# A two-layer graph attention and expert kernel: second-layer score terms over DRAM instead of TensorE, dense expert weights kept in SBUF

## The chip, the cores and the metric

The kernel runs on one core of a Trainium2 chip. The metric is the device time of one execution in microseconds (us). An execution with the hardware profiler gives a trace; its span runs from the first to the last instruction, and the execution's own time is a little longer. Engines: PE is TensorE (PEld its weight loads), DVE is VectorE, ACT is ScalarE, POOL is GpSimd, SP is SyncE, which here only issues DMAs. L523 is line 523 of the kernel before.

## The reference, cut to what matters

The input x is 64 batches of 256 rows of 256 numbers (float32). Two layers follow one another, each a graph attention and a feed-forward part, both added to x behind a layer norm.

```
x = x + gat0(layernorm(x))            # 4 heads of 64, slope 0.2, elu
x = x + layernorm(x) @ Wf.T + bf
x = x + gat1(layernorm(x))            # 1 head of 256, slope 0.01, relu
x = x + moe(layernorm(x))             # 8 experts, the best 2 of each row
```

In a graph attention h = x @ W, each row i has two numbers s_i = h_i.a1 and d_i = h_i.a2, and

```
e_ij = leaky_relu(s_i + d_j), masked by adj;   out_i = softmax_j(e_ij) @ h
```

The expert part gives each row the sum of two experts' gelu(x @ w1[e] + b1[e]) @ w2[e] + b2[e], weighted by a softmax over the two, plus the row itself.

## The kernel before, in words

Because exp(leaky_relu(s + d)) is the larger of two products of exponentials, the scores need no exponential per pair (i, j): for each source row j (a partition) a multiplication by masked factors and a maximum with a term that belongs to i and lies along the free dimension. The terms of the 256 rows i must therefore stand as a row of 256 numbers on all 128 partitions, while they are computed as a column, one per partition. This turn and spread is what the change is about.

Batches. A batch goes through `batch_layers` (L594): transposition, projection (L469), first-layer scores (`scores`, L559), weighted sum (`attended`, L576, PE pv L584), first feed-forward (PE pf L660, then DVE L667), second-layer projection (`projected1`, L497), scores (`scores1`, L520), weighted sum, second residual (DVE L694), norm, base rows (the residual and norm that the experts add to), router logits (PE pl L748). The first 61 batches are routed: in chunks (11 of 4 batches, 7 of 2, 3 of 1) their normed rows are sent by GpSimd's indirect DMAs (L1066) into regions of DRAM, one per expert. Full pairs of 128 rows of one expert (129 in all) are then loaded by SyncE (xr L906, xt L917, the expert's weights we L935), turned by VectorE (sT L117), go through PE ph L968, ACT hT L974, PE py L983, DVE y L993 and ACT y L961, and GpSimd adds them to the output by two indirect DMAs (L1004). Each pair's two scatters wait for the landing of the two before (L1001). The last three batches are dense: all 8 experts are computed for them (`dense_expert`, L1022), first for batch 61, then for 62 and 63 together, and each of these 16 jobs loads its expert's weights (L1026) into the same 7 buffers "we" as the pairs.

Order. The order on every engine is written out by a small planner (L1241). A job is a generator; each of its pieces ends with `yield rank`. In one step of the planner all active jobs go on by one piece, smallest rank first; a negative rank means that the next piece still belongs to this step. A new batch begins every three steps, so several batches are in flight at different places, and a rank decides what stands ahead of what on each engine. Engines work strictly in this order, and so does each DMA queue: a DMA that waits holds up all that are behind it on its queue.

The turn before. In the first layer (from batch 1) VectorE turns blocks of 32x32 of the exponentials (ut, L537), a DMA writes them to DRAM as one row (L621), and another reads that row onto all partitions (L554), into a part of the buffer that the maxima are then written to; from batch 18 (`SETTLED`) both are on SyncE's queue. In the second layer TensorE does it: two transpositions (L523) of the column, spread to 128 columns, give the row in PSUM, and the two maxima L528 read it there. Both stand at rank 25 of the step behind the projection; the weighted sum follows at rank 40 of the next step.

The values' scaling is DVE L485 (first layer, rank 24). It needs ACT's exponentials q L477.

Of the kernel before, what the change touches and what calls it, by code (L numbers as in the profile page):

```python
# [9 lines left out]
F32 = mybir.dt.float32  # L10
I32 = mybir.dt.int32
AF = mybir.ActivationFunctionType
ALU = mybir.AluOpType
AX = mybir.AxisListType

P = 128
# [5 lines left out]
def rows_to_all(ap: bass.AP, n: int) -> bass.AP:  # L22

    return bass.AP(tensor=ap.tensor, offset=ap.offset, ap=[[0, P], [1, n]])
# [3 lines left out]
def kernel(  # L28
# [17 lines left out]
    nc = tc.nc  # L46
    B, N, D = x.shape
# [3 lines left out]
    KT = D // P  # L51
    NT = N // P
# [16 lines left out]
    ROW = D + 4  # L69
# [3 lines left out]
    io = ctx.enter_context(tc.tile_pool(name="io", bufs=2))  # L73
    work = ctx.enter_context(tc.tile_pool(name="work", bufs=2))
    small = ctx.enter_context(tc.tile_pool(name="small", bufs=4))
    keep = ctx.enter_context(tc.tile_pool(name="keep", bufs=1))
    psum = ctx.enter_context(tc.tile_pool(name="psum", bufs=2, space=bass.MemoryType.PSUM))

    def bank(name, shape):
        t = psum.tile([P, 2 * D], F32, tag="bank", name=name, bufs=8)  # L80
        n = 1
        for s in shape:
            n *= s
        t = t[:, :n]
        if len(shape) == 2:
            t = t.rearrange("p (a b) -> p a b", a=shape[0])
        elif len(shape) == 3:
            t = t.rearrange("p (a b c) -> p a b c", a=shape[0], b=shape[1])
        return t
# [22 lines left out]
    S = 32  # L112
    G = P // S
# [15 lines left out]
    SETTLED = CHUNKS[0] + CHUNKS[1] + CHUNKS[2] + CHUNKS[3] + 2  # L129


    ident = const.tile([P, P], F32, tag="ident", name="ident")
# [138 lines left out]

    C_B1, WROW = KT * D, KT * D + 64
    WBUFS, XBUFS, YBUFS = 7, 5, 9
    wpack = tc.dram_tile([E, P, WROW], F32, name="wpack")
    w2s = const.tile([P, E, KT * D], F32, tag="w2s", name="w2s")
# [41 lines left out]
    def once(work):  # L319
# [14 lines left out]
        out=tri, in_=tri, pattern=[[1, P]], base=0, channel_multiplier=-1,  # L334
# [157 lines left out]
    for i in range(2):  # L492
        t = keep.tile([P, NT, D + 1], F32, tag=f"q1_{i}", name=f"q1_{i}")
# [3 lines left out]
    def projected1(xT, rstd, b):  # L497

        q = q1s[b % 2]
        pqs = []  # L500
        for t in range(NT):
            pq = bank("pq", [D + 3])
            for k in range(KT):
                nc.tensor.matmul(  # L504
                    pq, xT[:, k, t * P : (t + 1) * P], wx1[:, k, :],
                    start=(k == 0), stop=(k == KT - 1),
                )
            pqs.append(pq)
        ex = small.tile([P, NT, 3], F32, tag="ex1", name="ex1")
        for t, pq in enumerate(pqs):  # L510
            nc.scalar.activation(ex[:, t, :], pq[:, D:], AF.Exp, scale=rstd[:, t : t + 1])  # L511
            nc.scalar.activation(
                q[:, t, :D], pq[:, :D], AF.Copy, scale=rstd[:, t : t + 1]
            )
        me = work.tile([P, NT, N], F32, tag="me", name="me", bufs=1)
        for j in range(NT):
            nc.scalar.activation(me[:, j, :], masks[1][:, j, :], AF.Copy, scale=ex[:, j, 0:1])
        return q, ex, me

    def scores1(ex, me):  # L520
        pd = bank("pd", [N])
        for t in range(NT):
            nc.tensor.transpose(  # L523
                pd[:, t * P : (t + 1) * P], ex[:, t, 1:2].to_broadcast([P, P]), ident
            )
        z = work.tile([P, NT, N], F32, tag="z1", name="z1", bufs=1)
        for j in range(NT):
            nc.vector.scalar_tensor_tensor(  # L528
                z[:, j, :], pd, ex[:, j, 2:3], me[:, j, :], op0=ALU.max, op1=ALU.mult
            )  # L530
        return [z[:, j, :] for j in range(NT)]

    def send_terms(q, b):


        ut = small.tile([P, S], F32, tag="ut", name="ut", bufs=1)
        nc.vector.transpose(  # L537
            ut.rearrange("p (t h w) -> p t h w", t=NT, h=H), q[:, :, :, HD - 1 : HD + 3]
        )
        ud = tc.dram_tile([S, S], F32, name=f"terms_{b}")  # L540
        ud = ud.rearrange("c r -> (c r)").rearrange("(c p) -> c p", p=P)
        return ut, ud
# [51 lines left out]
    def batch_layers(b, c0, xng, lg):  # L594
# [23 lines left out]
        if b:  # L618
            ut, ud = send_terms(q, b)
            yield -31  # L620
            terms_queue(b).dma_start(  # L621
                out=ud.rearrange("c (g r) -> g c r", g=G),
                in_=ut[2 : P : S // (NT * H), :],
            )
            yield -52
        z = work.tile([P, NT, NT, H, P], F32, tag="z4", name="z4", bufs=2)
# [17 lines left out]
        ex = work.tile([P, NT, D], F32, tag="e", name="e", bufs=1)  # L644
# [21 lines left out]
        for t in range(NT):  # L666
            nc.vector.scalar_tensor_tensor(  # L667
                x2[:, t, :], pf[:, t, :], rstd[:, t : t + 1], x1b[:, t, :],
                op0=ALU.mult, op1=ALU.add, accum_out=sums[:, t : t + 1],
# [6 lines left out]
        xT = transposed(x2)  # L676
        yield 20
        q, ex, me = projected1(xT, rstd, b)
        yield 25
        z = scores1(ex, me)  # L680
        yield 40
        pvs, rinv = attended(
            q[:, :, None, :], 1, lambda j, h, t: z[j][:, t * P : (t + 1) * P]
# [9 lines left out]
        for t in range(NT):  # L693
            nc.vector.scalar_tensor_tensor(  # L694
                x2[:, t, :], x2[:, t, :], 1.0, rel[:, t, :],
                op0=ALU.mult, op1=ALU.add, accum_out=sums[:, t : t + 1],
# [36 lines left out]
        if not dense:  # L733
            d = nc.sync.dma_start(
                out=out_rows[b * N : (b + 1) * N, :].rearrange("(t p) d -> p t d", p=P), in_=base
# [18 lines left out]
            dense_batch[b] = dict(base=base, xT=xT)  # L754

    XNG = 8
    dense_batch = {}

    def dense_home(b):

# [203 lines left out]
    def hidden(xT, we):  # L964
        ph = bank("ph", [KT, PAIR])
        for f in range(KT):
            for k in range(KT):
                nc.tensor.matmul(  # L968
                    ph[:, f, :], we[:, k * D + f * P : k * D + (f + 1) * P], xT[:, k, :],
                    start=(k == 0), stop=(k == KT - 1),  # L970
                )
        hT = work.tile([P, KT, PAIR], F32, tag="hT", name="hT", bufs=5)
        for f in range(KT):
            nc.scalar.activation(  # L974
                hT[:, f, :], ph[:, f, :], AF.Gelu, bias=we[:, C_B1 + f : C_B1 + f + 1]
            )
        return hT

    def product(hT, e):
        py = bank("py", [2, D])  # L980
        for t in range(2):
            for f in range(KT):
                nc.tensor.matmul(  # L983
                    py[:, t, :], hT[:, f, t * P : (t + 1) * P],
                    w2s[:, e, f * D : (f + 1) * D].rearrange("p e c -> p (e c)"),
                    start=(f == 0), stop=(f == KT - 1),
                )
        return py
# [33 lines left out]
    def dense_expert(e, group):  # L1022

        yield 90
        we = io.tile([P, WROW], F32, tag="we", name="we", bufs=WBUFS)
        nc.sync.dma_start(out=we, in_=wpack[e])  # L1026
        yield 40
        for b in group:
            own = dense_batch[b]
            yield 35  # L1030
            hT = hidden(own["xT"], we)
            yield -85
            py = product(hT, slice(e, e + 1))
            for t in range(NT):
                for add in (py[:, t, :], b2s[:, e, :]):
                    nc.vector.scalar_tensor_tensor(
                        own["base"][:, t, :], add, own["w"][:, t, e : e + 1],
                        own["base"][:, t, :], op0=ALU.mult, op1=ALU.add,
                    )
            if e == E - 1:  # L1040
                begin(store_dense(b), 99)

    def store_dense(b):

        own = dense_batch[b]
        yield 99
        d = nc.sync.dma_start(
            out=out_rows[b * N : (b + 1) * N, :].rearrange("(t p) d -> p t d", p=P),
            in_=own["base"],
        )  # L1050
        tc.declare_no_dep(d.ins, query=SYNC, group="out", reason="no row is added to here")
        tc.add_to_no_dep_group("out", d.ins)
        nc.sync.nop()
# [6 lines left out]
    def begin(job, rank):  # L1060
        active.append([rank, len(order), job])
        order.append(job)
# [126 lines left out]
    def route_dense(b, lg):  # L1189

        c = len(CHUNKS) + 1 + b - ROUTED
        ohs, ed = in_one(top_two(c, NT, lg, chunk_tile([NT], "first", c)))
        yield 75
        two = chunk_tile([2, NT], "two", c)
        nc.scalar.activation(two[:, 0], ed, AF.Tanh, scale=-0.5)
        second_weight(two[:, 1], two[:, 0])
        nc.vector.tensor_tensor(two[:, 0], two[:, 0], two[:, 1], ALU.add)
        w = chunk_tile([NT, E], "wd", c, DENSE)
        nc.vector.tensor_tensor(
            ohs, ohs, two[:, :, :, None].to_broadcast([P, 2, NT, E]), ALU.mult  # L1200
        )
        nc.vector.tensor_tensor(w, ohs[:, 0], ohs[:, 1], ALU.add)
        dense_batch[b]["w"] = w
        for group in GROUPS:
            if b == group[-1]:
                dense_jobs.extend(
                    (len(group), lambda e=e, g=group: dense_expert(e, g)) for e in range(E)
                )
# [109 lines left out]
```

## Time and profile before

| | |
|---|---|
| median of 3 runs | 1486.39 us (1485.4 to 1491.55) |
| profiled execution, its own time | 1489.83 us |
| its span | 1488.0 us, mean granted TensorE clock 0.985 |
| busy: PE / PEld / DVE / ACT / POOL | 1420.1 / 1264.0 / 1232.9 / 1006.5 / 864.6 us |
| DMA | 236.10 MB, mean 159 GB/s |
| SyncE's queue (q1 with ACT's share) | 157.90 MB, 42.1% of 16 engines |
| GpSimd's queue (q0) | 66.33 MB, 23.9% |
| we<-wpack | 145 loads of 288 KB |
| pd<-ident,ex (L523) | 128 transpositions, mean 278 ns, 26.2 us |
| z<-pd,ex,me (L528) | 128 maxima, mean 460 ns, 53.8 us |

How to read it: busy time is the sum of what an engine's instructions took. TensorE's matmuls are pipelined and the ends of the pieces are modelled, so that pieces overlap; the distance from one start to the next tells what a piece holds. In lines of the timeline the columns are the start in us from the span's start, the length in us, engine, line, operation, output<-inputs, shape, count, and in brackets the idle time of the engine ahead of it with what ended it. SPq is SyncE's DMA queue; the length of its lines is the time of issue, not of the transfer. In lines of waits the columns are who waited for whom, the us in total, how often, and the longest.

### The profile page before, as it was taken

The page shows a single profiled execution, that of the slowest core. Times are in us where ns is not written, and L with a number is a line of the kernel's source. Part 1 is how long each engine was busy: PE and PEld are TensorE (multiplying, and loading weights), DVE is VectorE, ACT ScalarE, POOL GpSimd, SP SyncE. Part 2 cuts the span into 40 slices and gives each one's busy share as a digit, 9 for nine tenths or more (in the row PEclk, how much of TensorE's full clock was granted, in tenths as well). Part 3 has the DMA queues.
Part 4 walks back from the last instruction along what each step waited for, and adds up shares of the span by engine and source line. Part 5 has one row for each costly group of instructions (what it writes and reads, how often), then busy time and mean ns, then how long its engine had stood idle before and what let it go on. Part 6 is the DMA issues. An engine that isn't in the chain of part 4 may idle for free. (4 is left out here: it accounts for less than half of the span.)

```text
span 1488.0 us, 29865 instructions
## 1 busy us (share of the span) xinstructions
PE 1420.1 (95%) x8138; PEld 1264.0 (85%) x8138; DVE 1232.9 (83%) x4320; ACT 1006.5 (68%) x2389; POOL 864.6 (58%) x851
## 2 busy tenths in 40 slices
PE   6899999999999999999999999999999999899994
PEld 5688888898999999899999989888888888778883
DVE  7689999988898889899888989998888888765442
ACT  1377667577777777777777787777777878643330
POOL 2122446455857676666758585776666668544444
PEclk9899999999999999999999999999999999999998
DMA  4832243567878777787877687768877786988743
GB/s 128 227 98 86 89 130 117 146 172 153 199 171 193 161 177 170 171 185 180 190 156 190 147 193 168 190 164 186 193 158 172 153 173 128 213 201 150 152 66 49
DMA packets 354081, 236.10 MB, mean 159 GB/s; under 512 B 246260, under 2 KB 316156, under 8 KB 353916
## 3 DMA queue, kind: packets, MB, share of 16 engines
q1 hardware_dynamic: 301000, 157.90, 42.1%
q0 software_dynamic: 48864, 66.33, 23.9%
q10 hardware_dynamic: 4052, 9.98, 2.3%
q8 instruction: 67, 1.10, 0.3%
q14 instruction: 98, 0.80, 0.2%
HBM read 146.00 MB, written 88.09 MB: 157 GB/s over the span
## 5 line engine op out<-in xcount | busy, mean ns | idle before, releaser
L1004 POOL DMA_INDIRECT out_dram<-y,xt x258 | 415.6, 1611 | 214.6 <-issue 54.6
L584 PE MATMUL pv<-q,z 128*128 128x65 f32 (+1 forms) x2560 | 363.7, 297 | 0.7 <-DVE z L570 0.3
L584 PEld LDWEIGHTS pv<-q,z 128*128 128x128 f32 x2560 | 331.2, 193 | 13.3 <-DVE z L570 1.3
L1066 POOL DMA_INDIRECT xs<-xng,pos x244 | 256.3, 1050 | 65.2 <-issue 57.7
L983 PE MATMUL py<-w2s,hT 128*128 (+1 forms) x1224 | 282.9, 382 | 4.7 <-ACT hT L974 4.5
L983 PEld LDWEIGHTS py<-w2s,hT 128*128 128x128 f32 x1224 | 229.7, 191 | 37.2 <-ACT hT L974 7.4
L570 DVE SCALAR_TENSOR_TENSOR z<-z,q,mask 128x256 f32<-128x256 f32 x504 | 231.5, 482 | 15.5 <-DMA z<-terms 6.5
L968 PE MATMUL ph<-sT,we 128*128 128x256 f32 x1032 | 241.4, 383 | 1.6 <-DVE sT L117 0.9
L968 PEld LDWEIGHTS ph<-sT,we 128*128 128x128 f32 x1032 | 195.6, 192 | 28.7 <-DVE sT L117 1.4
L961 ACT ACTIVATE y<-y,w 128x256 f32<-128x256 f32 x258 | 113.4, 499 | 119.4 <-DVE y L993 119.2
L459 ACT COPY xT<-pt 128x512 f32<-128x512 f32 x209 | 121.2, 588 | 82.1 <-PE pt L453 80.0
L974 ACT ACTIVATE hT<-ph,we 128x256 f32<-128x256 f32 x306 | 124.1, 472 | 64.1 <-PE ph L968 46.7
L406 POOL TENSOR_SCALAR rstd<-mv 128x4 f32<-128x4 f32 (+1 forms) x66 | 15.9, 240 | 224.8 <-DVE mv L379 175.3
L504 PE MATMUL pq<-wx,xT 128*128 128x259 f32 x512 | 126.5, 390 | 13.9 <-ACT xT L459 13.9
L424 ACT ACTIVATE off<-x,sums 128x256 f32<-128x256 f32 x256 | 129.2, 505 | 9.2 <-DVE x L667 3.3
L993 DVE TENSOR_TENSOR y<-py,b2s 128x512 f32<-128x512 f32 x129 | 86.9, 687 | 56.3 <-PE py L983 44.8
L469 PE MATMUL pq<-wx,xT 128*128 128x268 f32 x512 | 128.1, 394 | 2.4 <-DVE xT L117 1.2
L504 PEld LDWEIGHTS pq<-wx,xT 128*128 128x128 f32 x512 | 96.0, 192 | 33.6 <-ACT xT L459 19.8
L660 PE MATMUL pf<-wfT,xT 128*128 128x256 f32 x512 | 124.2, 386 | 0.0
L469 PEld LDWEIGHTS pq<-wx,xT 128*128 128x128 f32 x512 | 97.9, 192 | 21.7 <-DVE xT L117 1.4
L688 ACT ACTIVATE rel<-pv,rinv 128x256 f32<-128x256 f32 x128 | 54.0, 469 | 82.1 <-DVE rinv L591 81.8
L660 PEld LDWEIGHTS pf<-wfT,xT 128*128 128x128 f32 x512 | 94.9, 196 | 10.6
(170 smaller groups left out, 2355.7 us busy)
## 6 DMA issues: line engine op xcount, KB each, us to landing
we<-wpack SPq DMA_DIRECT2D x145, 288.0 KB
xr<-xs SPq DMA_DIRECT2D x516, 64.0 KB
z<-terms SPq DMA_DIRECT2D x46, 512.0 KB
xin<-in_x_dram SPq DMA_DIRECT2D x64, 256.0 KB
out_dram<-base SPq DMA_DIRECT2D x61, 256.0 KB
xblk<-in_x_dram SPq DMA_DIRECT2D x188, 64.0 KB
z<-terms ACTq DMA_DIRECT2D x17, 512.0 KB
out_dram<-y,xt POOLq DMA_INDIRECT x258
```

The costliest lines, as they stand in the source:

```text
L424: nc.scalar.activation(off, src[:, t, :], AF.Square, bias=sums[:, t : t + 1], scale=-float(D), accum_out=sq[:, at + t : at + t + 1],)
L459: nc.scalar.copy(dst, pt)
L469: nc.tensor.matmul(pq.rearrange("p h c -> p (h c)"), xT[:, k, t * P : (t + 1) * P], wx[:, k, :], start=(k == 0), stop=(k == KT - 1),)
L504: nc.tensor.matmul(pq, xT[:, k, t * P : (t + 1) * P], wx1[:, k, :], start=(k == 0), stop=(k == KT - 1),)
L570: nc.vector.scalar_tensor_tensor(z[:, j, :, h, :], terms, q[:, j, h, HD + 2 : HD + 3], masks[0][:, j, :].rearrange("p (t i) -> p t i", t=N ...
L584: nc.tensor.matmul(pv[:, h, :], z(j, h, t), q[:, j, h, : d + 1], start=(j == 0), stop=(j == NT - 1),)
L660: nc.tensor.matmul(pf[:, t, :], xT[:, k, t * P : (t + 1) * P], wfT[:, k, :], start=(k == 0), stop=(k == KT - 1),)
L968: nc.tensor.matmul(ph[:, f, :], we[:, k * D + f * P : k * D + (f + 1) * P], xT[:, k, :], start=(k == 0), stop=(k == KT - 1),)
L974: nc.scalar.activation(hT[:, f, :], ph[:, f, :], AF.Gelu, bias=we[:, C_B1 + f : C_B1 + f + 1])
L983: nc.tensor.matmul(py[:, t, :], hT[:, f, t * P : (t + 1) * P], w2s[:, e, f * D : (f + 1) * D].rearrange("p e c -> p (e c)"), start=(f == 0 ...
L1004: d = nc.gpsimd.indirect_dma_start(out=out_rows, out_offset=bass.IndirectOffsetOnAxis(ap=xt[:, t, 0:1].bitcast(I32), axis=0), in_=y[:, t, ...
L1066: d = nc.gpsimd.indirect_dma_start(out=xs_d[: E * CAP * PAIR, :], out_offset=bass.IndirectOffsetOnAxis(ap=at, axis=0), in_=xe, in_offset=None,
```

## The change

Three things are changed.

1. Second layer, from batch 18: VectorE turns the terms (`turned_terms1`, rank 23 of the projection's step, ahead of the values' scaling at 24), SyncE writes 1 KB to DRAM (rank 27) and reads it onto all partitions, 128 KB, into the last part of the maxima's buffer (rank 32). The maxima read it there and stand at rank 62 of the next step, behind the second residual (rank 60), where they stood at rank 25. Batches up to 17 keep the transpositions and rank 25.
2. Dense weights: each expert's weights are loaded once and kept, in the 8 buffers "xng" in which routed batches' rows were kept; the second group of dense batches uses them again. 8 loads in place of 16, of 514 columns.
3. A packed row of weights in DRAM has 528 columns where it had 576; the pairs' loads are of whole packed rows.

ScalarE's and GpSimd's orders of instructions are unchanged. On TensorE only the 46 pairs of transpositions are missing. On VectorE 46 turns are new and 46 pairs of maxima have moved. On SyncE 92 DMAs are new and 8 are missing.

```diff
-    C_B1, WROW = KT * D, KT * D + 64
+    C_B1, WROW = KT * D, KT * D + 16
...
-    def scores1(ex, me):
-        pd = bank("pd", [N])
-        for t in range(NT):
-            nc.tensor.transpose(
-                pd[:, t * P : (t + 1) * P], ex[:, t, 1:2].to_broadcast([P, P]), ident
-            )
-        z = work.tile([P, NT, N], F32, tag="z1", name="z1", bufs=1)
+    def turned_terms1(ex, b):
+
+        ut = small.tile([P, S], F32, tag="ut1", name="ut1", bufs=1)
+        nc.vector.transpose(
+            ut.rearrange("p (t w) -> p t w", t=NT),
+            ex[:, :, 1:2].to_broadcast([P, NT, S // NT]),
+        )
+        return ut, tc.dram_tile([N], F32, name=f"terms1_{b}")
+
+    def scores1(ex, me, z, spread):
+
+        terms = z[:, NT - 1, :]
+        if not spread:
+            terms = bank("pd", [N])
+            for t in range(NT):
+                nc.tensor.transpose(
+                    terms[:, t * P : (t + 1) * P], ex[:, t, 1:2].to_broadcast([P, P]), ident
+                )
         for j in range(NT):
             nc.vector.scalar_tensor_tensor(
-                z[:, j, :], pd, ex[:, j, 2:3], me[:, j, :], op0=ALU.max, op1=ALU.mult
+                z[:, j, :], terms, ex[:, j, 2:3], me[:, j, :], op0=ALU.max, op1=ALU.mult
             )
...
         q, ex, me = projected1(xT, rstd, b)
-        yield 25
-        z = scores1(ex, me)
+        spread = b >= SETTLED
+        if spread:
+            yield -23
+            ut, ud = turned_terms1(ex, b)
+            yield -27
+            nc.sync.dma_start(
+                out=ud.rearrange("(t g r) -> g t r", t=NT, g=G),
+                in_=ut[0 : P : S // NT, :],
+            )
+            yield -32
+        z = work.tile([P, NT, N], F32, tag="z1", name="z1", bufs=1)
+        if spread:
+            nc.sync.dma_start(out=z[:, NT - 1, :], in_=rows_to_all(ud, N))
+        yield 62 if spread else 25
+        z = scores1(ex, me, z, spread)
         yield 40
...
-        we = io.tile([P, WROW], F32, tag="we", name="we", bufs=WBUFS)
-        nc.sync.dma_start(out=we, in_=wpack[e])
+        if e not in dense_weights:
+            we = keep.tile([P, NT, ROW], F32, tag="xng", name=f"wd_{e}", bufs=XNG)
+            we = we.rearrange("p t c -> p (t c)")[:, : C_B1 + KT]
+            nc.sync.dma_start(out=we, in_=wpack[e, :, : C_B1 + KT])
+            dense_weights[e] = we
+        we = dense_weights[e]
```

More of the change, by code (lines that the diff above doesn't have):

```diff
@@ L756 @@
     XNG = 8
-    dense_batch = {}
+    dense_batch, dense_weights = {}, {}
     def dense_home(b):
```

## The prediction, as it was put on record

> **What bounds the kernel now.** I read in this order: the busy time of each engine by stretch (which engine is full, and where), the timeline of TensorE over one batch (its rhythm), those of VectorE and SyncE over the same batch (what room the new work finds), and GpSimd's timeline to the end.
>
> By stretch the columns are us, then busy time (and count) of PE, PEld, DVE, ACT, POOL, then clock, DMA share, GB/s:
>
> ```profile
> 300.00:400.00 100.00, 100.00 (x596) 90.56 (x595) 89.55 (x303) 76.70 (x182) 62.39 (x62) 1.00 0.71 171
> ...
> 500.00:600.00 100.00, 100.00 (x598) 90.64 (x597) 89.32 (x306) 76.75 (x183) 63.96 (x62) 1.00 0.77 171
> ...
> 900.00:1000.00 100.00, 96.17 (x573) 86.03 (x572) 92.18 (x335) 72.93 (x173) 67.44 (x66) 1.00 0.71 166
> ...
> 1100.00:1200.00 100.00, 99.69 (x567) 88.08 (x565) 86.90 (x313) 79.46 (x173) 68.32 (x61) 1.00 0.77 165
> ```
>
> TensorE is full from 300 to 900 us; the list of waits has no TensorE wait there at all, and 11.4 us of them from 900 to 1255 (8.1 behind ACT xT L459 in 5 places, 2.8 behind DVE x L667, 0.5 in small ones). One batch of the timeline of TensorE:
>
> ```profile
> 707.52 3.62 PE L983 MATMUL py<-w2s,hT 128*128 x16
> 710.98 0.38 PE L523 MATMUL pd<-ident,ex 128*128 128x128 f32 x2
> 711.20 3.68 PE L584 MATMUL pv<-q,z 128*128 128x65 f32 x32
> ```
>
> Each piece starts before the last one's modelled end: only start to start counts. The two transposes L523 hold their place from 710.98 to 711.20. In 35 of the 46 batches concerned this distance is 218 or 219 ns; the distance from one such pair to the next is 19.90 us, or 20.35 with a chunk's routing.
>
> The end belongs to GpSimd. Its timeline:
>
> ```profile
> 1255.24 0.19 POOL L444 TENSOR_SCALAR rstd<-sq 128x4 f32<-128x4 f32 x1 [1.23 <-ACT off L424]
> ...
> 1277.01 1.57 POOL L1004 DMA_INDIRECT out_dram<-y,xt  x1 [4.69 <-DMA xr<-xs]
> ...
> 1471.03 1.63 POOL L1004 DMA_INDIRECT out_dram<-y,xt  x1 [3.60 <-DMA out_dram<-y,xt]
> 1472.97 1.56 POOL L1004 DMA_INDIRECT out_dram<-y,xt  x1 [0.30 <-issue]
> 1478.34 1.56 POOL L1004 DMA_INDIRECT out_dram<-y,xt  x1 [3.81 <-issue]
> 1480.20 1.56 POOL L1004 DMA_INDIRECT out_dram<-y,xt  x1 [0.30 <-issue]
> ```
>
> At 1255.24 GpSimd waits for the batches for the last time. After that it is late: each pair's two adding scatters wait for the landing of the pair before, and the last pair, whose values ACT had scaled at 1447.7, goes out at 1478.3. So the last 230 us are a chain of their own that starts when the batches let it; what TensorE gains before about 1255 moves it forward as a whole.
>
> **The change part by part.** *Transposes.* From batch 18 the pair L523 goes: 46 pairs, from about 326 us on. The group has a mean of 278 ns; 92 of them by busy time would be 25.6 us, but that counts overlap twice. By start to start it is 46 x 0.218 = 10.0 us. [...] I take 10.0, less about six savings (1.3) that stand ahead of a wait between 900 and 1255 and are eaten by it, less 0.4 for the last two batches, behind 1255: 8.3.
>
> *VectorE.* Added: 46 turns of 128x32. Nearest row: ut L537, 212 ns. Where it lands:
>
> ```profile
> 707.58 0.18 DVE L379 BATCH_NORM_AGGREGATE mv<-stats 128x2 f32<-128x6 f32 x1
> 708.32 0.88 DVE L485 SCALAR_TENSOR_TENSOR q<-pq,rstd,q 128x256 f32<-128x256 f32 x2 [0.56 <-ACT q L477]
> ```
>
> It stands just ahead of L485 (the values' scaling), where VectorE waits 0.56 us for ACT's second exponentials; its own input, ex L511, was done at 706.97. It costs nothing under that cover, and 0.21 x 46 = 9.8 us if the cover were gone and VectorE the bound. The maxima L528 stay two per batch; they read SBUF where they read PSUM. [...] The same line L570 measured both ways here says 482 ns from SBUF against 471 from PSUM: 1.0 us more in all. I take the row; VectorE has 2 us free per batch, so 0.
>
> Moved: the maxima go from ahead of rinv L591 and hp L639 to behind the second residual L694. What comes next on VectorE is x2 L667, and the sum up to it is unchanged; before, L667 waited 0.6 us on average for PE pf in 23 of the batches to 900 anyway. rinv comes 0.8 us sooner and may wait up to 0.4 us for PE pv; that takes the place of this wait. The user of the maxima, PE pv of this layer, starts at 721.69, 4 us behind. Near the end the cover is thinner: in batch 61 rinv already waits (1.5 us), so the maxima stand in L667's way there: +0.7 us.
>
> *Two DMAs a batch on SyncE's queue.* Nearest rows: the first layer's own terms on the same queue.
>
> ```profile
> 709.48 0.55 SPq L621 DMA_DIRECT2D terms<-ut  x1
> 710.07 0.45 SPq L96 DMA_DIRECT2D xin<-in_x_dram  x1
> 712.38 0.35 SPq L554 DMA_DIRECT2D z<-terms  x1
> ```
>
> Packets of the trace: the write is down 1.38 us after its issue begins, the read can begin 1.73 us after it, and the 512 KB read ends 4.7 us (median, longest 5.7) after its own. The new read is 128 KB: eight 1 KB packets per DMA engine at 65 to 88 ns are 0.7 us after a start at 1.1, so 1.8 from below, 4.7 from above (another shape behind a busy queue); I take 2.5, nearer the small transfer. Turn to landing: 0.2 + 1.7 + 2.5 = 4.4 us, at most 6.6. The time there is: exponent done (706.97) to the maxima's new place (716.3), 9.3 us; 8.6 in the tightest batch to 900, 7.7 after. It fits with 1 to 4 us to spare. Only in batch 63 is it 5.2 us: up to 1.4 us of stall, once.
>
> On the queue the write waits for VectorE's turn, the read for the write. Behind them stand the first layer's write and read, xin, the base's store and the loads of two pairs. The first layer's write waits for VectorE 1.3 us later than the new one, so the wait for landing lies beside it; the rest is issue, 0.55 + 0.35 and gaps, 1.0 us per batch. The queue stood 7.2 us per batch waiting for VectorE:
>
> ```profile
> SPq L621 <- DVE stats L378: 321.8, 45, 11.9
> ```
>
> So 0. In batches 61 to 63 no first layer is left and the new write is the wait: batch 63's holds the queue until its exponent at 1282.1, and pair loads issued between 1273 and 1293 come up to 11 us later. The first of them was turned by VectorE at 1295.2; from issue at about 1284.5 it needs 3.4 us of issue and about 4.5 of landing: still 2.8 early. 0, with 3 as the upper bound.
>
> *Packed rows.* 576 to 528 columns, 8% fewer bytes for 129 loads. No TensorE wait names we, so 0.
>
> *Dense weights.* Sixteen loads of 288 KB on SyncE become eight, in the buffers of the sent rows. At 1302 those of the early ones are long free, and the last buffer's user (batch 63) is through at about 1320, 30 us before its load was issued (1350). TensorE runs without a break from 1317 to 1450, so no load was waited for. What is gained is traffic: four of the eight dropped loads (1357 to 1397) lie beside scatters that follow one another at 6.5 to 7.7 us, against 6.3 to 6.5 with nothing beside. Between 0 and 4 x 1.0 us; I take 1.5, since the pairs' own loads stay.
>
> Sum: -8.3 + 0.7 - 1.5 = -9.1. The profiled execution took 1489.83 (span 1488.0), 3.4 over the median of 1486.39; after, such an execution would be 1480.7 and the median 1477.3, so **1477**.
>
> **Rivals.**
> - *More than that* (0.10): the weights and shorter rows free the scatters by up to 4 us and the waits of 900 to 1255 shrink rather than eat: -10.0 - 4 gives 1472.
> - *GpSimd already sets the pace earlier* (0.30, within 0.5%). From about 1123 the scatters lag the scaled values by a steady 14 to 21 us. If they are the chain from there, only (1123 - 326)/20.5 = 39 savings count, less four eaten: 7.6; with 0.7 and up to 3 of stalls at the end given back and nothing from traffic, 1479 to 1484. Against it: GpSimd waits for ACT at 1231.44 and 1255.24.
> - *The terms arrive too late* (0.14, slower). Place: the maxima behind the read, on VectorE in order. It decides from a turn-to-landing of 8.6 us; with VectorE's 2 us of room and TensorE's 0.22 spent, from about 10.8 us the kernel is slower, by 44 us for each further us: 11.0 gives 1495, 11.5 gives 1517. The trace's worst sum for the larger transfer, 0.2 + 2.6 + 5.7 = 8.5, is just short; against it, that xin's packets and the pair loads share the queue's 16 engines, at 0.77 busy.
> - *Own range of the likeliest* (0.46): 1471 to 1482.
>
> **Numbers.** A measurement of this kernel cannot tell 0.5% (7.4 us) from no change, so faster means below 1479.0. The likeliest case lies below that for 0.44 of its 0.46, with the 0.10 of the first rival and 0.02 of the second: 0.56. Within: 0.02 + 0.27 = 0.29, and slower 0.15, the third rival and 0.01 of the second. The range leaves out about 0.05 below and 0.14 above: 1467 to 1495.
>
> **What would show it.** Right: pitch from batch to batch 19.68 where it was 19.90, TensorE still full to 900, no wait of L528's successor on the terms, ut1 in the place of the 0.56, the last GpSimd wait for the batches near 1246, the scatters at 6.5 us from about 1390 on. Wrong: VectorE waits named z<-terms at the maxima (third rival), TensorE waits behind DVE or ACT at an unchanged 19.90 pitch, or a gain in the batches that GpSimd's chain does not hand on (second).

## The result and the profile after

The changed kernel took 1482.38 us (median of 22 runs, 1477.99 to 1490.42), the kernel before on the same chip in the same hour 1489.35 (22 runs, 1480.22 to 1497.85). The ratio is 0.995, 95% interval [0.9936, 0.9963]. The profiled execution has a span of 1483.7 us where before had 1488.0. It took 1485.5 us, 3.1 over the median of its kernel; that of before took 1489.83, 0.5 over.

Some lines have moved: L504 (second layer's projection), L485, L511 and L453 are unchanged; L523 is now the new turn, and the old L523 pair is L535; the maxima are L539, rinv L602, the second residual L718, x2 L678, PE pv L595, PE py L1007, the scatters L1028; the new write and read are L695 and L702.

Busy time by stretch, after (columns as in the prediction):

```profile
300.00:400.00 100.00, 100.00 (x593) 90.69 (x592) 90.96 (x309) 77.39 (x183) 62.40 (x63) 1.00 0.72 176
...
1100.00:1200.00 100.00, 99.91 (x558) 87.65 (x557) 89.13 (x319) 82.05 (x180) 68.47 (x62) 1.00 0.80 171
```

TensorE is as full as before up to 900 us, with fewer instructions in each stretch: it does a batch in less time. VectorE has taken on 1.4 and 2.2 us in 100. The rhythm, in TensorE's timeline, before:

```profile
703.53 1.91 PE L504 MATMUL pq<-wx,xT 128*128 128x259 f32 x8
723.43 1.92 PE L504 MATMUL pq<-wx,xT 128*128 128x259 f32 x8
743.72 1.97 PE L504 MATMUL pq<-wx,xT 128*128 128x259 f32 x8
```

and after:

```profile
697.82 1.91 PE L504 MATMUL pq<-wx,xT 128*128 128x259 f32 x8
717.50 1.91 PE L504 MATMUL pq<-wx,xT 128*128 128x259 f32 x8
737.56 1.97 PE L504 MATMUL pq<-wx,xT 128*128 128x259 f32 x8
```

Start to start it is 19.68 and, with a chunk's routing, 20.06, where the same two steps were 19.90 and 20.29: 0.22 or 0.23 less. And the new work, in the timeline of all engines over the same batch:

```profile
710.68 1.01 DVE L539 SCALAR_TENSOR_TENSOR z<-z,ex,me 128x256 f32<-128x256 f32 x2
...
721.74 0.19 DVE L523 STREAM_TRANSPOSE ut<-ex 128x32 f32<-128x32 f32 x1
721.96 0.55 SPq L695 DMA_DIRECT2D terms<-ut  x1
722.39 0.88 DVE L485 SCALAR_TENSOR_TENSOR q<-pq,rstd,q 128x256 f32<-128x256 f32 x2 [0.46 <-ACT q L477]
724.20 0.35 SPq L702 DMA_DIRECT2D z<-terms  x1
```

The turn stands ahead of L485, which still waits 0.46 us for ACT behind it: the turn cost nothing here. The write is issued 0.22 us after the turn begins and the read 2.24 us after the write. VectorE's list of waits (us in total, times, longest us) says what became of the room. Before:

```profile
DVE q L485 <- ACT q L477: 31.7, 39, 2.9
...
DVE x L667 <- PE pf L660: 22.6, 34, 1.7
...
DVE rinv L591 <- PE pv L584: 5.6, 8, 1.5
```

After:

```profile
DVE q L485 <- ACT q L477: 21.7, 38, 1.5
DVE rinv L602 <- PE pv L595: 16.2, 27, 1.6
...
DVE x L678 <- PE pf L671: 6.2, 8, 1.6
DVE ut L523 <- ACT ex L511: 5.8, 5, 1.6
...
DVE z L539 <- DMA z<-terms: 0.2, 1, 0.2
```

The turns fill part of the time in which L485 waited. rinv waits longer, since the maxima no longer stand ahead of it; x2's wait for PE pf is shorter by more than that. The terms were late once, in batch 63, by 0.2 us.

So the batches in which TensorE is full went as foreseen. The later ones brought no more in this trace. GpSimd, from the end of the batches to the end of the kernel:

```profile
1225.52 0.33 POOL L444 TENSOR_SCALAR rstd<-sq 128x4 f32<-128x4 f32 x1 [1.03 <-ACT off L424]
...
1249.66 0.19 POOL L444 TENSOR_SCALAR rstd<-sq 128x4 f32<-128x4 f32 x1
...
1474.30 1.55 POOL L1028 DMA_INDIRECT out_dram<-y,xt  x1 [3.98 <-issue]
```

The instruction that came at 1255.24 after a wait of 1.23 us now comes at 1249.66 after none, so that the last wait for a batch in this trace is the one at 1225.52. The two are 5.9 us (from 1231.44) and 5.6 us earlier than before, the last pair of scatters only 4.0. A second trace of the same kernel ("whole change again" below) does have the wait at this place, so its absence does not belong to the kernel as such:

```profile
1246.94 0.19 POOL L444 TENSOR_SCALAR rstd<-sq 128x4 f32<-128x4 f32 x1 [0.31 <-ACT off L424]
```

### The profile page after: what moved, and what is told of

Read it like the earlier page. It is cut to its first block, busy times and chain, and to the rows that moved or that the text cites. A ratio compares the mean times of both kernels' runs of the same rounds, so it can differ in the third digit from the quotient of the medians.

```text
span 1483.7 us, 29895 instructions
## 1 busy us (share of the span) xinstructions
PE 1416.2 (95%) x8046; PEld 1260.5 (85%) x8046; DVE 1240.3 (84%) x4366; ACT 1005.5 (68%) x2389; POOL 861.9 (58%) x851
## 5 line engine op out<-in xcount | busy, mean ns | idle before, releaser
L1028 POOL DMA_INDIRECT out_dram<-y,xt x258 | 414.2, 1605 | 229.8 <-issue 67.6
L595 PE MATMUL pv<-q,z 128*128 128x65 f32 (+1 forms) x2560 | 363.2, 297 | 0.3
L595 PEld LDWEIGHTS pv<-q,z 128*128 128x128 f32 x2560 | 333.5, 193 | 14.1 <-DVE z L581 0.4
L1007 PE MATMUL py<-w2s,hT 128*128 (+1 forms) x1224 | 284.3, 383 | 6.0 <-ACT hT L998 4.5
L1007 PEld LDWEIGHTS py<-w2s,hT 128*128 128x128 f32 x1224 | 230.4, 191 | 38.9 <-ACT hT L998 7.1
L504 PE MATMUL pq<-wx,xT 128*128 128x259 f32 x512 | 129.0, 395 | 13.2 <-ACT xT L459 13.2
L504 PEld LDWEIGHTS pq<-wx,xT 128*128 128x128 f32 x512 | 97.6, 195 | 32.6 <-ACT xT L459 18.1
L998 ACT ACTIVATE hT<-ph,we 128x256 f32<-128x256 f32 x258 | 104.1, 472 | 31.0 <-PE ph L992 26.5
L671 PEld LDWEIGHTS pf<-wfT,xT 128*128 128x128 f32 x512 | 94.6, 195 | 10.6
```

Source lines behind the costliest of these rows:

```text
L504: nc.tensor.matmul(pq, xT[:, k, t * P : (t + 1) * P], wx1[:, k, :], start=(k == 0), stop=(k == KT - 1),)
L595: nc.tensor.matmul(pv[:, h, :], z(j, h, t), q[:, j, h, : d + 1], start=(j == 0), stop=(j == NT - 1),)
L671: nc.tensor.matmul(pf[:, t, :], xT[:, k, t * P : (t + 1) * P], wfT[:, k, :], start=(k == 0), stop=(k == KT - 1),)
L1007: nc.tensor.matmul(py[:, t, :], hT[:, f, t * P : (t + 1) * P], w2s[:, e, f * D : (f + 1) * D].rearrange("p e c -> p (e c)"), start=(f == 0 ...
L1028: d = nc.gpsimd.indirect_dma_start(out=out_rows, out_offset=bass.IndirectOffsetOnAxis(ap=xt[:, t, 0:1].bitcast(I32), axis=0), in_=y[:, t, ...
```

## Experiments

Stages are measured between the starts of TensorE's L504 (or its counterpart) in batches 18, 46 and 63 of each trace, and from there to the start of the trace's last instruction. The kernels of one job ran on one chip. In three jobs the kernel before took 1487 to 1489 us, in the two marked with a star 1506; rows of the two kinds can't be subtracted from each other. Half clock is the time from batch 46 to 63 in which the granted TensorE clock was halved. The stages are those of one execution each, and leave out the start: batch 18 begins at 319.4 to 323.2 us in the 14 traces (323.2 before, 321.6 after, 319.4 in the whole change again), in no order of the kernels.

| kernel | ratio to before | interval | 18 to 46 | 46 to 63 | of it half clock | 63 to end |
|---|---|---|---|---|---|---|
| before | | | 560.4 | 393.9 | 6.8 | 210.6 |
| after | 0.995 | 0.9936 to 0.9963 | 554.2 | 396.1 | 13.7 | 211.8 |
| whole change again | 0.9958 | 0.9943 to 0.9974 | 554.2 | 394.3 | 10.2 | 210.9 |
| transposes beside | 1.0008 | 0.9993 to 1.0023 | 560.3 | 397.1 | 10.2 | 211.3 |
| terms left out | 0.9941 | 0.9922 to 0.9961 | 554.2 | 394.0 | 10.2 | 210.3 |
| late: turns on TensorE, maxima moved | 0.9941 | 0.9921 to 0.9961 | 554.2 | 392.2 | 6.8 | 210.0 |
| waits filled, second | 0.9973 | 0.9962 to 0.9984 | 554.2 | 397.2 | 6.8 | 214.8 |
| terms alone * | 1.0005 | 0.999 to 1.002 | 566.1 | 410.2 | 23.9 | 207.2 |
| dense alone * | 0.9994 | 0.9974 to 1.0014 | 571.7 | 401.9 | 13.7 | 208.8 |
| terms to batch 45 * | 0.996 | 0.994 to 0.998 | 567.9 | 404.7 | 17.1 | 205.6 |
| maxima at their old rank * | 1.0018 | 1.0002 to 1.0033 | 568.4 | 408.8 | 17.1 | 205.8 |
| waits filled, first * | 0.9977 | 0.9957 to 0.9997 | 567.4 | 399.0 | 10.2 | 214.4 |
| dense alone again * | 0.9991 | 0.9973 to 1.0009 | 568.1 | 400.5 | 10.2 | 210.1 |
| terms alone again * | 1.0004 | 0.9982 to 1.0025 | 564.5 | 404.9 | 20.5 | 211.3 |

My theory to begin with: TensorE's instruction stream sets the pace up to batch 45, and something that the change adds takes the gain of the later batches. The rival: TensorE isn't what bounds the later batches, and gains there are not handed on.

**The parts apart (job 1).** Terms alone leaves `WROW` and the dense loads as they were:

```diff
-    C_B1, WROW = KT * D, KT * D + 16
+    C_B1, WROW = KT * D, KT * D + 64
...
-        if e not in dense_weights:
...
-        we = dense_weights[e]
+        we = io.tile([P, WROW], F32, tag="we", name="we", bufs=WBUFS)
+        nc.sync.dma_start(out=we, in_=wpack[e])
```

> Only the second layer's terms go over DRAM; dense weights and packed rows as before. Theory (the gain is TensorE's missing transposes in the full stretch): pitch 19.68 up to batch 45, so about 6 us less there, and the whole change's gain, 1482 within noise, ratio 0.994 to 0.997. Rival (the gain is the dense weights' and the rows'): ratio 0.999 to 1.001. Rival (dense weights loaded once cost time at the end): faster than the whole change, 0.991 to 0.993.

Dense alone keeps TensorE's turns and rank 25 everywhere:

```diff
-        spread = b >= SETTLED
+        spread = False
```

> Only dense weights once and the narrower packed rows; terms turned by TensorE in all batches. Theory: pitch stays at 19.90, ratio 0.999 to 1.001, and the dropped loads show no faster scatters, since the pairs' loads only move forward. The prediction's step: 1.5 us gained, ratio 0.998 to 1.000. Rival (dense weights are the gain): ratio 0.994 to 0.997.

Terms to batch 45 only:

```diff
-        spread = b >= SETTLED
+        spread = SETTLED <= b < 46
```

> The whole change, but from batch 46 on TensorE turns the second layer's terms again and the maxima stand at rank 25. Theory (behind batch 46 TensorE is no longer full, the savings are eaten by waits that the moved maxima lengthen): not slower than the whole change, ratio to before 0.991 to 0.995, and TensorE's waits from batch 48 on back at about 20 us from 24. Rival (the late batches gain as predicted, 3 to 4 us): 2 to 4 us slower than the whole change, ratio 0.996 to 0.998.

The terms over DRAM, with the maxima at their old rank:

```diff
-        yield 62 if spread else 25
+        yield 25
```

> The whole change, but the maxima of the spread batches stay at rank 25, ahead of rinv and hp. The time for the terms shrinks by 1.8 us, and the trace shows 2.0 to 3.6 us of margin up to batch 52 and 0.4 to 2.1 behind 56. Theory: no change up to batch 45 (pitch 19.68, margin 0.2 to 1.8); behind it the maxima wait up to 1.4 us for the terms in some batches but rinv's wait for PE pv goes back: within 2 us of the whole change either way. Rival (the rank is what makes the change work): maxima wait in most batches, pitch above 19.9, ratio above 1.0.

Terms alone was expected at 0.994 to 0.997 and gained nothing; dense alone came as expected. Against dense alone, from the same chip, terms alone is 5.6 us shorter in batches 18 to 45 and 8.3 longer in 46 to 62 (the two differ in the dense part too). With the maxima at their old rank 3.3 us are saved and 6.9 given back; there the maxima waited for the terms in 14 places, 11.2 us in all, 9.2 of it from batch 46 on, and the ratio is above 1.0 as its rival had it.

The run that ends the trip at batch 45 has a ratio of 0.996: outside the 0.991 to 0.995 of its theory and at the edge of its rival's, which rested on a late gain that no run shows. Its median, 1499.01, is some 9 us below the 1508.35 and 1508.2 of the two runs beside it that send the late batches' terms over DRAM too, and the intervals don't touch. Each of these two differs from it in one more point (dense part, rank of the maxima), but the late trip is what they share: on this chip it seems to cost more than the turns on TensorE that it replaces. The whole change was not run beside them.

This chip hid some of the saving, too: TensorE, which in the first chip's traces waits nowhere from 320 to 900 us, does so here in both of the first two kernels. From TensorE's list of waits for dense alone:

```profile
PE pq L504 <- ACT xT L459: 5.8, 10, 1.5
```

**The transposes alone (job 2).** The whole change was run once more, and beside it a kernel that still makes the 46 pairs on TensorE, into a bank that nobody reads:

> The whole change once more, beside the other three on one chip, so that stages can be subtracted without a difference between chips. If the gain of 0.5% is the change's own, the ratio is 0.995 to 0.998 here too, with batches 18 to 45 shorter by 5 to 7 us than with the turns on TensorE, and nothing won or up to 6 us lost from batch 46 on. If it was peculiar to the first chip, the ratio is 1.000 and above.

```diff
-        terms = z[:, NT - 1, :]
-        if not spread:
-            terms = bank("pd", [N])
-            for t in range(NT):
+        terms = bank("pd", [N])
+        for t in range(NT):
...
+        if spread:
+            terms = z[:, NT - 1, :]
```

> The whole change, but TensorE goes on making its 46 pairs of turns from batch 18 on, into a bank that nobody reads; the maxima still take the terms that went over DRAM. Theory (TensorE's instruction stream sets the pitch of batches 18 to 45): those 28 batches get 28 x 0.218 = 6 us longer than in the whole change and the time rises by 6 to 10 us. Rival (the gain of batches 18 to 45 comes from the dense weights' rows, or from the maxima being moved, and TensorE had room): 0 to 2 us longer. From batch 46 on the theory says 0 to 4 us longer; should TensorE not be the bound there at all, 0.

The whole change gave 0.9958 and the transposes took all of it back: 1.0008. The medians are 9.2 us apart. Batches 18 to 45 went from 554.2 to 560.3, 6.1 us, 28 x 0.218; from 46 to 63 this trace is longer by 2.8. The timeline of TensorE with the unread pair has the old rhythm:

```profile
700.73 1.91 PE L504 MATMUL pq<-wx,xT 128*128 128x259 f32 x8
...
712.21 0.38 PE L533 MATMUL pd<-ident,ex 128*128 128x128 f32 x2
...
720.63 1.91 PE L504 MATMUL pq<-wx,xT 128*128 128x259 f32 x8
```

19.90 us again, though this kernel has the new turns, the DMAs, the moved maxima and the shorter rows. So up to batch 45 the gain is the TensorE work that was taken away, and nothing else.

**What takes the late gain?** First the trip itself. This kernel has no turn and no DMA for the second layer's terms from batch 18 on; its maxima take a constant mask in place of the terms, so the scores of those batches are other numbers:

```diff
-        terms = z[:, NT - 1, :]
+        terms = masks[1][:, NT - 1, :]
...
-            ut, ud = turned_terms1(ex, b)
...
-            nc.sync.dma_start(out=z[:, NT - 1, :], in_=rows_to_all(ud, N))
```

> The whole change, but from batch 18 on the second layer's terms are left out: no turn on VectorE, no write and no read over DRAM; the maxima take a constant in their place, at the same point. What the trip costs is the whole change less this run. Theory (the trip is hidden; the late batches give the gain back because the maxima stand behind the second residual and because of other waits): within 2 us of the whole change, in each stretch. Rival (turns on VectorE or transfers in SP's queue are what costs in the late batches): 3 to 8 us shorter from batch 46 on.

0.9941 against 0.9958, with intervals that overlap, and the same 554.2 and 394 us in the traces: up to batch 45 the trip is hidden, and behind it no cost of it can be told on this chip (the median is 1.7 us lower without it). Next the place of the maxima:

```diff
-        spread = b >= SETTLED
+        spread = SETTLED <= b < 46
...
-        yield 62 if spread else 25
+        yield 62 if b >= SETTLED else 25
```

> The terms go over DRAM for batches 18 to 45 only; from batch 46 on TensorE turns them again as before, but the maxima stay behind the second residual, the one thing in which this differs from the run in which the late batches were wholly as before (ratio 0.996). Theory (it is the place of the maxima that costs in the late batches): batches 46 to 62 lose 3 us or more against that run, ratio 0.998 or above. Rival (the place costs nothing, it is the trip or the clock): the ratio stays at 0.996.

My expectation failed. With the maxima moved and TensorE turning again in the 18 late batches (18 x 0.218 = 3.9 us of its stream), the kernel is not slower than the whole change; it has the lowest median of its job, 1478.45 us (6 runs) against 1480.89 (17). The place of the maxima is not what costs. Nor did the late transposes cost anything here, though this run also leaves out the late trip. The four kernels of this chip, side by side for batches 46 to 63:

| from batch 46 on | terms over DRAM | not over DRAM |
|---|---|---|
| turns on TensorE | 397.1 | 392.2 |
| no turns on TensorE | 394.3 | 394.0 |

With the trip the turns cost 2.8 us, without it nothing. These are single traces and differences of 2 us, so they do not settle whether TensorE's stream bounds the late batches. What can be read is where TensorE's time went from 46 to 63. Waits are the time in which it does nothing; half of the time at half clock is counted as lost (two projections took 1.68 us longer under 3.41 us of it, as shown below):

| kernel | 46 to 63 | waits | lost at half clock | the rest |
|---|---|---|---|---|
| before | 393.9 | 16.7 | 3.4 | 373.7 |
| after | 396.1 | 18.7 | 6.8 | 370.5 |
| whole change again | 394.3 | 18.4 | 5.1 | 370.8 |
| late: turns on TensorE, maxima moved | 392.2 | 15.5 | 3.4 | 373.3 |
| waits filled, second | 397.2 | 14.7 | 3.4 | 379.1 |

The late pairs did leave the stream: the rest is 2.9 to 3.2 us less than before. Waits of TensorE took back 1.6 to 2.0 of it and the half clock 1.7 to 3.4.

**The clock.** One more suspect was visible. Ahead of batch 54, TensorE in the whole change (second run) has lost 0.218 us of work, so its wait for xT is longer by about as much: 2.46 us, against 2.20 before and in the last kernel and 2.23 with the transposes beside. And then its clock is halved:

```profile
1048.98 3.27 PE L504 MATMUL pq<-wx,xT 128*128 128x259 f32 x8 [2.46 <-ACT xT L459]
1052.05 2.45 PE L469 MATMUL pq<-wx,xT 128*128 128x268 f32 x8
1054.33 0.60 PE L453 MATMUL pt<-ident,x 128*128 128x128 f32 x4
```

Start to start the two projections take 5.35 us in place of 3.67. The longer wait alone doesn't explain it: the clock was halved behind the 2.23 us too, but not behind the 2.20 nor behind 2.32 with the terms left out. To test whether this is where the gain went, two kernels fill TensorE's long waits with throw-away turns of the identity, into a bank that the next matmul overwrites:

```diff
...
+            for _ in range({53: 12, 54: 6, 62: 10}.get(b, 0) * (t == 0)):
+                nc.tensor.transpose(pq[:, :P], ident, ident)
...
-        xT = transposed(x2)
+        xT = transposed(x2, fill={61: 22, 63: 10}.get(b, 0))
```

> The whole change, and at five of TensorE's longest waits in the late batches it makes throw-away turns of the identity (12, 6, 22, 10 and 10 of them, 0.109 us each by the pairs of 0.218, which is 1.3, 0.7, 2.4, 1.1 and 1.1 us) into the bank that the next real matmul overwrites, so that each wait shrinks to 1.0 to 1.4 us. Theory (a TensorE idle for some 2 us of a 3.41 us stretch runs the next 3.41 us at half clock, and this gives the late gain back): of the half-clock stretches between batch 46 and the start of batch 63, 3 or 4 in the two profiles of the whole change (10.2 and 13.7 us), none or one is left; each that goes saves up to 1.7 us, so the time falls 3 to 5 us below the whole change's, ratio 0.992 to 0.994. Rival (the half clock only lies beside other waits and costs nothing, or the throw-away turns come in the way): the ratio stays at 0.9955 or rises.

This first one was misplaced (batch 53 has no long wait) and fell on the slower kind of chip, without the whole change beside it. Its 0.9977 lies on the side of its rival and decides nothing. In the same job the two parts were run again:

> Dense weights loaded once and the packed rows' stride alone, the same kernel as before on another chip. Theory (this part is worth nothing): ratio 0.999 to 1.001. Rival (my sum's 1.5 us through faster scatters): 0.9985 or below.

> The terms' part alone, the dense weights loaded each time as before; the same kernel as before on another chip. On the first of its chips it gained nothing (1.0005) though batches 18 to 45 were 5.6 us shorter. Theory (chance and that chip's own waits took it): here 0.995 to 0.997, batches 18 to 45 at a pitch of 19.79 us. Rival (without the dense part the late batches always give it back): 0.999 and above.

Both repeat the first job: dense alone 0.9991, terms alone 1.0004, although the terms shorten batches 18 to 45 there by 3.6 us. The expected 0.995 to 0.997 failed. The second filling is `{50: 6, 51: 10, 54: 12, 55: 6, 62: 10}` and `{61: 22, 63: 22}`:

> As the first run with filled waits, with the throw-away turns where they belonged: that run put 12 of them at batch 53, where the wait was short, and only 6 at batch 54, where 1.93 us of waiting were left and the half clock came all the same; at batch 63 10 left 2.63 us. Now 6, 10, 12, 6 and 10 ahead of the second layer's projections of batches 50, 51, 54, 55 and 62, and 22 ahead of the second layer's transposes of batches 61 and 63. Theory: no wait of over 1.9 us is left at these places and no half-clock stretch follows one of them; from batch 46 to the start of batch 63 none or one is left. Beside the two profiles of the whole change with 10.2 and 13.7 us of half clock there, that is worth 3 to 6 us: on a chip where the kernel before takes some 1487 us, ratio 0.992 to 0.994; on one where it takes some 1506 us, at most 0.9965. Rival (the half clock lies beside waits that cost the same without it): ratio as the whole change, 0.9955 to 0.996 on the first kind of chip, 0.9977 or more on the second.

At batch 54 it does what it should. The timeline of TensorE:

```profile
1047.28 1.47 PE L506 MATMUL pq<-ident 128*128 128x128 f32 x12
1049.88 2.02 PE L508 MATMUL pq<-wx,xT 128*128 128x259 f32 x8 [1.13 <-ACT xT L461]
1051.74 1.97 PE L471 MATMUL pq<-wx,xT 128*128 128x268 f32 x8
1053.55 0.60 PE L455 MATMUL pt<-ident,x 128*128 128x128 f32 x4
```

The clock stays full, and batches 53 and 54 take 26.77 and 25.61 us where they took 27.03 and 27.29: 1.94 us won on TensorE, which is what before took there (26.55 and 25.82). Yet the ratio is 0.9973, no better than the whole change and far from the expected 0.992 to 0.994: that the clock took the gain is not borne out by the time. In the split above the rest, which holds the throw-away turns, is 8.3 us more than in the whole change again, where waits and half clock fell by 5.4. In this trace, of an execution 4.2 us over the median of its kernel, the advance is gone at batch 61, where TensorE waits for x2, and x2 for GpSimd. The timeline of all engines:

```profile
1214.35 1.60 POOL L1032 DMA_INDIRECT out_dram<-y,xt  x1 [3.96 <-issue]
...
1217.89 0.24 POOL L406 TENSOR_SCALAR rstd<-mv 128x2 f32<-128x2 f32 x1
...
1218.97 0.48 DVE L682 SCALAR_TENSOR_TENSOR x<-pf,rstd,x1b 128x256 f32<-128x256 f32 x1 [7.41 <-POOL rstd L407]
...
1219.52 1.12 PE L455 MATMUL pt<-ident,x 128*128 128x128 f32 x4 [5.40 <-DVE x L682]
```

rstd stands on GpSimd behind two scatters, and the first scatter waits 3.96 us. The same place, TensorE alone, before:

```profile
1224.54 1.09 PE L453 MATMUL pt<-ident,x 128*128 128x128 f32 x4 [2.77 <-DVE x L667]
```

and in after:

```profile
1213.45 1.60 POOL L1028 DMA_INDIRECT out_dram<-y,xt  x1 [1.71 <-DVE z L539]
...
1216.99 0.23 POOL L406 TENSOR_SCALAR rstd<-mv 128x2 f32<-128x2 f32 x1
...
1218.07 0.48 DVE L678 SCALAR_TENSOR_TENSOR x<-pf,rstd,x1b 128x256 f32<-128x256 f32 x1 [3.82 <-POOL rstd L407]
...
1218.61 0.84 PE L453 MATMUL pt<-ident,x 128*128 128x128 f32 x4 [3.83 <-DVE x L678]
```

TensorE waits there in each trace: 2.8 us before, 3.8 in after, 3.6 in the whole change again, 6.5 with the terms left out, 5.4 here on top of 2.6 of throw-away turns, 2.1 in the kernel whose late turns TensorE makes itself. What releases that scatter is not named in this trace ("issue"), and the releaser differs between traces of one order of instructions; I can't say why it is late. Whether the filling itself costs time stays open too: that run was on another chip than the whole change, and the intervals (0.9962 to 0.9984, and 0.9943 to 0.9974) overlap.

## Why the prediction was right, and where not

*TensorE's in-order stream, 0.218 us a pair:* right to the hundredth. (By the trace the distance is 218 or 219 ns in 38 of the 46 batches; the prediction has 35, which changes no sum.) The pitch went from 19.90 to 19.68, and putting the pairs back restored it.

*The transposes' term of 8.3 us:* too large. It stands for 6.1 in batches 18 to 45 and 2.2 in the later ones, after what waits eat. The first part came (560.4 to 554.2). The second did not: from 46 to 63 the profile after is 2.2 us longer than before, that of the whole change again 0.4. The prediction charged 1.3 for savings that stand directly ahead of a wait and nothing for the clock; by the split of TensorE's time it was 1.6 to 2.0 of waits and 1.7 to 3.4 of half clock.

*The rivals.* The prediction's times were laid from a median before of 1486.39, and before measured 1489.35 in the comparison. Taken as gains, the measured 7.0 us lies in the range of the likeliest case (4.4 to 15.4) and in that of the rival in which GpSimd sets the pace earlier (2.4 to 7.4); the time can't tell them apart. The signs don't either. GpSimd's last wait for a batch is at 1225.52 in after, which speaks for the rival, but at 1246.94 in the whole change again, where the likeliest case had it. And TensorE's waits for x2, which GpSimd's rstd holds up, are no longer in sum from 46 to 63: 5.9 us before, 5.9 after, 5.4 again. That GpSimd takes the late gain is not shown. That the total came within 2 us of the forecast 9.1 owes something to luck: the late 2.2 us and the dense 1.5 us are not seen in the runs.

*Dense weights, 1.5 us:* not shown. The two runs alone give 0.9994 and 0.9991, or 0.9 and 1.4 us, with intervals that reach from a gain of 4 us to a loss of 2. The mechanism is not seen: the pairs of scatters numbered 108 to 128 took 138.8 us before, 140.5 after and 138.0 in the whole change again. The dense loads that remain come closer together (DMA share 0.99 from 1300 to 1350 in after where it was 0.88).

*VectorE's turn, the packed rows, the queue: 0 each:* right up to batch 45, where the stage stays 554.2 us with turn and transfers taken away. For the later batches it holds on that chip within the interval, and seems not to on the chip of the first job.

*Maxima moved, 0.7 us in batch 61:* rinv did wait longer, 10.6 us more over all, but it took the place of x2's wait, which fell by 16.4, as the step said; a cost of the move could not be measured.

*Maxima from SBUF, 11 ns each:* the wrong cost. A pair takes 1.00 us after (0.83 before); at the same place it takes 0.87 where the late batches read PSUM again (late: turns on TensorE) and 0.88 with the terms left out, where the maxima read a constant in SBUF. So the source hardly matters. What costs is that the second maxima write over the terms that both read: in the trace they wait for a semaphore that the first ones raise, and with PSUM or the constant they don't. From the start of the first to that of the second it is 516 ns (median), against 397 with the constant and 363 before. That is 0.13 us a batch on VectorE, hidden up to batch 45, as was the turn. In the timelines of before, after and the terms left out:

```profile
714.82 0.83 DVE L528 SCALAR_TENSOR_TENSOR z<-pd,ex,me 128x256 f32<-128x256 f32 x2
...
710.68 1.01 DVE L539 SCALAR_TENSOR_TENSOR z<-z,ex,me 128x256 f32<-128x256 f32 x2
...
709.71 0.88 DVE L539 SCALAR_TENSOR_TENSOR z<-mask,ex,me 128x256 f32<-128x256 f32 x2
```

*The terms' trip, 4.4 us from turn to landing:* about 5.1 by the trace. Write to read took 2.2 us (median) where I had 1.7; the read landed 2.7 us after its issue where I had 2.5. In batch 63 the maxima waited 0.2 us for it, where the prediction allowed 1.4. The rival in which the terms come too late is out for the whole change.

The sum that the runs support is the -6.1 of batches 18 to 45: the ratio 0.9958 of 1487.5 us is a gain of 6.2, and 0.995 of 1489.35 one of 7.4 (between 5.5 and 9.5), so that what lies beyond it is within the noise.

*What stays open:* what in the late batches turns the saving into waits, and why the late trip seems to cost some 9 us on the first job's chip and at most a few on that of the second. On the chips where before takes 1506 us the terms alone gained nothing (1.0005 and 1.0004), although their full stretch was shorter there too; the whole change was not run on such a chip without fillings. Half-clock time from 46 to 63 is 10 us higher in both of those traces than in dense alone beside them, which fits up to 5 us of loss, but the second filling did not bear that out, and it is not shown.

## What to carry to other kernels

Count what is taken from a full, in-order engine by its distances from start to start, and only over the stretch in which nothing makes that engine wait; put the pieces back beside the change to prove it. Where an engine is 99% busy but waits a few times, a saving can come back as waiting: split its time into waits, lost clock and the rest, before and after. Make such a change only where it pays: the two runs that kept it to batches 18 to 45 gained about as much as the whole change (0.996 and 0.9941 against 0.995 and 0.9958). A difference of 2 us in one stage of a profile can be chance between two executions, so let medians on one chip decide it, and take a sign from two traces before believing it.

## What the runs showed of the hardware

The clock. Half-clock stretches last 3.41 us or a multiple of it (but for the one that the end of the trace cuts) and begin on a grid of 3.413 us in each trace (residuals of 2 ns). Cutting all 14 traces by their own grid between 890 and 1260 us, and leaving aside stretches that were at half clock themselves: in each of the 31 that were followed by half clock TensorE had been idle for 1.93 us or more, and in none of the others for more than 1.98. The least of these idle times, 1.93 us, is 57% of a stretch. So a wait of 2.2 us may cost nothing or some 1.7 us, by where it falls on the grid: ahead of batch 54 it cost nothing before (2.20) and 1.7 with the transposes beside (2.23). At batch 54 filling the wait with throw-away transposes, which left 1.13 us of it, kept the clock.

The chips. The same kernel took 1487 to 1489 us in three jobs and 1506 in two. In the traces of the slower kind, where VectorE's rinv waits for its PE pv between 320 and 880 us, it begins mostly 1 to 2 us after the modelled end of PE pv, and ACT's copy of a transposition (xT) is as late behind its own in most batches; in the other kind both begin 0.04 us after it. Why, the records don't show.
